# Rank-8 channel scales multiplied as float32r passes, with both operands split in two parts

## The chip, the cores and the metric

The kernel runs on one core of a Trainium2 chip. The core has a matrix engine (TensorE, PE in the profile, with its weight loads shown as PEld), a vector engine (VectorE, DVE), an activation engine (ScalarE, ACT), a general engine (GpSimd, POOL) and SyncE (SP), which here only issues DMAs. Each engine works through its own queue in order and waits on semaphores for the others. The metric is the device time of one execution in microseconds (us); smaller is better.

## The reference

The program takes hidden states x of 4 batches of 512 rows with 1024 features. It normalizes each row, runs causal attention with rotary embedding (16 heads of 64), and multiplies the result by a gate. The gate is a one-layer network with a sign-valued weight whose inputs and outputs are scaled per token and channel; the scales are what the change is about:

```python
xf = x.reshape(-1, H)
router_logits = xf @ gate_w.T
routing = jax.nn.softmax(router_logits.astype(jnp.float32), axis=1).astype(x.dtype)
in_scale = routing @ in_channel_scale
out_scale = routing @ out_channel_scale
wb = ste_sign(weight)
out = xf * in_scale @ wb.T * out_scale + bias
```

The output is `x + attention(xn) * silu(out)`, with `xn` the normalized rows in both places. Each scale matrix is thus a product with a contraction over only eight experts.

## The kernel before

**Stages.** The first and longest stage runs over 16 groups k, that is 4 batches b times 4 groups g of four heads. In each group the projections of query, key and value (`project`, L260, a Strassen scheme of seven products) are interleaved on PE with the attention pieces of the group before: scores, softmax, transposes of the probabilities (`transpose_p`, L432), values. Pieces that belong to other work are put between them: the router in each batch's first group, the sign of two weight blocks there too, the normalization and transposes of the next batch's rows in groups 2 and 3. After that come two units of the gate's feed-forward beside the last attention pieces, and then, for each of the eight units q (a unit is two row blocks of 128, `pairs`), the output projection `project_out(q)` and the feed-forward `gated(q + 1)` in turn.

**Who sets the order.** PE's order is as written (`tc.manual_schedule(engines={PE})`, L69). On the other engines a scheduler of the framework orders the instructions by its own estimate of when they can run; the first batch's opening is written out for DVE and ACT too (L618). Buffers come from pools: a new tile waits until the older tile in its slot has been read. A pool that matters here is `xin` (L113), two row buffers of 128x1024 shared by the next batch's rows (`load_x`) and the weight blocks whose sign is taken (`load_sign`). The PSUM ring (L116) has four banks for products, transposes and scales alike.

**The router** (L471) works per batch in three steps that stand apart in PE's order. Step 0: logits on PE, eight expert columns in a field of 32 for each row block, copied out by ACT (`lgs`). Step 1: a transpose, then maximum, subtraction, exponential (ACT), sum, reciprocal and product (`rex`, L494 to L502); the 24 unused columns of each field are zeroed by POOL (L492). Step 2: a transpose back on PE (L508), a copy (`rT`), and four stores of eight rows by SP to a DRAM tile `rt_d` (L512).

**The scales.** `load_xn(q)` (L535) fetches a unit's normalized rows and its routing `RT[q]`: eight rows of routing in each of the four 32-partition groups, by four SP DMAs (L548). `isc` and `osc` hold the two scale tables, eight rows in each of the four partition groups (L686, L687, loaded early by eight SP DMAs). `in_scales(q)` (L560) makes 16 products of 8x128 by 8x128, four channel blocks j on the four partition groups, and DVE multiplies the rows by them (L577). `split(q)` (L579) takes the scaled rows apart into two float32r tiles, `HI` and `LO`, for the feed-forward (L777). `out_scales(q)` (L592) makes four products of 8x128 by 8x512; ACT copies them out (L606). Both run in float32.

For units 0 and 1 these products stand inside the last four attention groups, where they use the score banks; for units 2 to 7, inside `project_out` of the unit before:

```python
            ahead = [
                lambda: (in_scales(q + 1), split(q + 1)),
                lambda: None,
                lambda: out_scales(q + 1),
            ]
```

On POOL, which the change gives new work, stand the scaling of the probabilities (L400), two steps of the rotary embedding (L253, L254), one addition of the projections (L336), and in the last stage the bias, gate and residual additions (L788, L797, L901, L921) and the output DMAs (L925, L928).

Of the kernel before, what the change touches and what calls it, by code (L numbers as in the profile page):

```python
# [9 lines left out]
F32 = mybir.dt.float32  # L10
F32R = mybir.dt.float32r
AF = mybir.ActivationFunctionType
ALU = mybir.AluOpType
AX = mybir.AxisListType
# [6 lines left out]
B, S, E = 4, 512, 1024  # L21
H, D = 16, 64
NE = 8
P = 128
# [4 lines left out]
TPB = S // P  # L29
HALF = 512  # L30
# [21 lines left out]
def attn_gated_ffn_kernel(  # L52
# [14 lines left out]
    nc = tc.nc  # L67
# [3 lines left out]
    cp = ctx.enter_context(tc.tile_pool(name="const", bufs=1))  # L71
    st = ctx.enter_context(tc.tile_pool(name="stats", bufs=4))
    sgp = ctx.enter_context(tc.tile_pool(name="sign", bufs=1))
    dp = ctx.enter_context(tc.tile_pool(name="spill", bufs=1, space=DRAM))
# [6 lines left out]
        out=mask,  # L81
        in_=mask,
        compare_op=ALU.is_ge,
        fill=MASK_VAL,
        base=0,
        pattern=[[-1, P]],
        channel_multiplier=1,
# [7 lines left out]
    gw = cp.tile([P, NC, 32], F32, name="gw")  # L95
    nc.gpsimd.memset(gw, 0.0)

    isc = cp.tile([P, E], F32, name="isc")
    osc = cp.tile([P, E], F32, name="osc")

    xn_d = dp.tile([B, TPB, P, E], F32, name="xn_d")
    at_d = dp.tile([B, TPB, P, E], F32, name="at_d")

    rt_d = dp.tile([B, TPB, NE, P], F32, name="rt_d")
    sg = [sgp.tile([P, E], F32R, name=f"sg{n}") for n in range(NC)]


# [3 lines left out]
    xip = ctx.enter_context(tc.tile_pool(name="xin", bufs=2))  # L113
    rtp = ctx.enter_context(tc.tile_pool(name="rt", bufs=2))
# [354 lines left out]
    R = {}  # L469

    def router(b, step):  # L471
        if step == 0:
            lg = bank(f"lg_{b}")[:, :P]
            for c in range(NC):
                for t in range(TPB):
                    nc.tensor.matmul(
                        lg[32 * t : 32 * t + 32, :],
                        lhsT=gw[:, c, :],
                        rhs=X[b][:, c, t * P : (t + 1) * P],
                        start=(c == 0),  # L480
                        stop=(c == NC - 1),
                    )
            R["lg"] = st.tile([P, P], F32, tag="r", name=f"lgs_{b}", bufs=2)
            nc.scalar.copy(R["lg"], lg)
        elif step == 1:
            lt = bank(f"lt_{b}")[:, :P]
            nc.tensor.transpose(lt, R["lg"], ident)
            ltg = lt.rearrange("p (t e) -> p t e", e=32)[:, :, :NE]
            nmx = st.tile([P, TPB], F32, tag="rmx", name=f"rmx_{b}")
            nc.vector.tensor_reduce(nmx, ltg, AX.X, ALU.max)  # L490
            ex = st.tile([P, TPB, 32], F32, tag="r", name=f"rex_{b}", bufs=2)
            nc.gpsimd.memset(ex, 0.0)  # L492
            exv = ex[:, :, :NE]
            nc.vector.tensor_tensor(  # L494
                exv, ltg, nmx[:, :, None].to_broadcast((P, TPB, NE)), op=ALU.subtract
            )
            nc.scalar.activation(exv, exv, AF.Exp)
            ssum = st.tile([P, TPB], F32, tag="rsum", name=f"rsum_{b}")
            nc.vector.tensor_reduce(ssum, exv, AX.X, ALU.add)
            rs = st.tile([P, TPB], F32, tag="rrs", name=f"rrs_{b}")  # L500
            nc.vector.reciprocal(rs, ssum)
            nc.vector.tensor_tensor(  # L502
                exv, exv, rs[:, :, None].to_broadcast((P, TPB, NE)), op=ALU.mult
            )
            R["ex"] = ex
        else:
            rt = bank(f"rt_{b}")[:, :P]
            nc.tensor.transpose(rt, R["ex"].rearrange("p t e -> p (t e)"), ident)  # L508
            rT = st.tile([P, P], F32, tag="r", name=f"rT_{b}", bufs=2)
            nc.vector.tensor_copy(rT, rt)  # L510
            for t in range(TPB):
                nc.sync.dma_start(out=rt_d[b, t], in_=rT[32 * t : 32 * t + NE, :])  # L512


    staged = {}

    def load_sign(n):
        staged[n] = xip.tile([P, E], F32, tag="x", name=f"wb_{n}")
        nc.sync.dma_start(out=staged[n], in_=wb[n // 4, n % 4])

    def make_sign(n):

# [12 lines left out]
    def load_xn(q):  # L535
        b, t = pairs[q]
        if q < 2:
            if q == 0:
                XP["first"] = xp.tile([P, 2, 2, NC, P], F32, tag="X", name="xp_01")
            XP[q] = XP["first"][:, q]  # L540
        else:
            XP[q] = xsp.tile([P, 2, NC, P], F32, tag="xp", name=f"xp_{q}")
        for i in range(2):
            nc.sync.dma_start(out=XP[q][:, i].rearrange("p c q -> p (c q)"), in_=xn_d[b, t + 2 * i])

        RT[q] = rtp.tile([P, 2, P], F32, tag="rt", name=f"rt_{q}")
        for j in range(4):
            nc.sync.dma_start(  # L548
                out=RT[q][32 * j : 32 * j + NE, :, :],
                in_=rt_d[b, t : t + 3 : 2].rearrange("t e p -> e t p"),  # L550
            )

# [6 lines left out]

    def in_scales(q, banks=ring_banks):  # L560

        ps = [v.rearrange("p (i r q) -> p i r q", i=2, r=2) for v in banks(f"is_{q}")]
        for r in range(2):
            for i in range(2):
                for j in range(4):
                    p0, c = 32 * j, 4 * r + j
                    nc.tensor.matmul(  # L567
                        ps[j][:, i, r, :],
                        lhsT=isc[p0 : p0 + NE, c * P : (c + 1) * P],
                        rhs=RT[q][p0 : p0 + NE, i, :],  # L570
                        start=True,
                        stop=True,
                    )
        by_j = XP[q].rearrange("p i (r j) q -> p i r j q", j=4)
        for j in range(4):
            xs = by_j[:, :, :, j, :]
            nc.vector.tensor_tensor(xs, xs, ps[j], op=ALU.mult)  # L577

    def split(q):  # L579

# [11 lines left out]
    def out_scales(q, banks=ring_banks):  # L592
        ps = banks(f"os_{q}")
        for n in range(4):
            i, k = n // 2, n % 2
            nc.tensor.matmul(
                ps[n],
                lhsT=RT[q][32 * n : 32 * n + NE, i, :],
                rhs=osc[32 * n : 32 * n + NE, k * HALF : (k + 1) * HALF],
                start=True,  # L600
                stop=True,
            )
        for n in range(4):
            i, k = n // 2, n % 2
            Z[q, i] = z_place[q % 2][i]
            nc.scalar.copy(Z[q, i][:, k * HALF : (k + 1) * HALF], ps[n])  # L606
# [73 lines left out]
    for k, (b, g) in enumerate(groups):  # L680
        pieces = []
        if k > 0:
            pieces, late = attention_pieces(k - 1, late)
        if k == 1:
            for t in range(TPB):
                nc.sync.dma_start(out=isc[32 * t : 32 * t + NE, :], in_=in_scale)  # L686
                nc.sync.dma_start(out=osc[32 * t : 32 * t + NE, :], in_=out_scale)  # L687
        extra = []
        if g == 0:
            extra = [lambda s=s: router(b, s) for s in range(3)]  # L690
        elif g == 1 and b + 1 < B:
            for t in range(2):
                load_x(b + 1, t)
        elif g > 1 and b + 1 < B:
            t0 = 2 * (g - 2)
            for t in range(t0, t0 + 2):
                layernorm(b + 1, t)
            extra = [
                lambda t=t, h=h: transpose_x(b + 1, t, h) for t in range(t0, t0 + 2) for h in range(2)
            ]  # L700
            if g == 2:
                extra.append(lambda: [load_x(b + 1, t) for t in (2, 3)])
        if g == 0:
            extra += [
                lambda: (load_sign(2 * b), load_sign(2 * b + 1)),
                lambda: None,
                lambda: make_sign(2 * b),
                lambda: make_sign(2 * b + 1),
            ]

        step = max(1, (len(pieces) + len(extra)) // (len(extra) + 1))
        for n, e in enumerate(extra):
            pieces.insert(min(len(pieces), (n + 1) * step + n), e)
        if b == B - 1:

            if g < 2:
                load_xn(g)
            if g in (1, 2):
                pieces.insert(3, lambda: in_scales(g - 1, score_banks))
            if g == 3:  # L720
                z_place[0] = [xip.tile([P, E], F32, tag="x", name=f"z0_{i}") for i in range(2)]
                pieces.insert(3, lambda: out_scales(0, score_banks))
        fill = project(b, g) if k else first
        interleave(pieces, fill, 3 * 7 * 4)
        if g == NGRP - 1 and b + 1 < B:
            for n in (1, 2, 3, 4):
                form_x(b + 1, n)
# [88 lines left out]
    w, v = late  # L816
# [193 lines left out]
```

## Time and profile before

| what | us |
|---|---|
| median of 3 runs | 1217.93 (1216.91 to 1218.15) |
| the profiled execution | 1218.51 |
| its span, first to last instruction | 1216.7 |
| in-scale products (L567), 256 records, from start to next matmul at 701.45 | 1.11 |
| out-scale products (L596), 64 records, the same at 806.42 | 1.07 |
| DVE multiplication by the in-scales (L577), one of 32 | 0.68 |
| ACT copy of the out-scales (L606), one of 32, four per unit | 0.60 |
| SP's issue of a routing load (L548), median of 32 | 0.29 |
| SP's issue of a routing store (L512), median of 16 | 0.29 |
| POOL's issue of an output DMA (L925, L928), 16 | 0.57 to 0.77 |

A float32 matmul of the program leaves two records in the trace, a float32r matmul one. A row of the timeline gives the start, the duration of what it merges, the engine, the line, the operation, the tiles and their sizes, and in brackets how long the engine stood idle before it and what released it. Matmuls are pipelined, so their cost is read from one start to the next and not from a record's length.

### The profile page before, as it was taken

The numbers are of one execution on the slowest core, as the hardware profiler recorded it, in microseconds if no ns is written. First come the engines' busy times: TensorE is split into PE (matmuls) and PEld (weight loads), VectorE is DVE, ScalarE is ACT, GpSimd is POOL, SyncE is SP. The second block draws the span as 40 slices with busy tenths as digits, with TensorE's granted clock in tenths as the row PEclk, the third lists the DMA queues.
The fourth block names the chain that finished last, engine by engine and source line by source line (L and its number), as shares of the span: only waits on it lengthen the run. The fifth ranks groups of instructions, "written<-read, shape, count | busy, mean of one in ns | idle before, by whom it ended". The sixth has DMA issues, their size and how long they took to land.

```text
span 1216.7 us, 18118 instructions
## 1 busy us (share of the span) xinstructions
PE 1184.6 (97%) x6920; PEld 897.6 (74%) x6920; DVE 742.2 (61%) x1364; ACT 500.1 (41%) x1142; POOL 526.4 (43%) x566
## 2 busy tenths in 40 slices
PE   6999998999999899999999999999999999999997
PEld 5988887887888788787887888788664546655663
DVE  7775758766665867666786666665675343444432
ACT  3553745446374544447454443545432121212110
POOL 0463436344343545344363524535445434533543
PEclk9999999999999999999999999999999999999999
DMA  8413324122233422214234221210515423341320
GB/s 301 144 70 113 102 90 147 48 75 81 88 111 95 131 79 78 79 48 142 89 100 161 79 78 44 87 45 27 192 33 194 138 72 102 105 139 35 104 70 34
DMA packets 56983, 120.27 MB, mean 99 GB/s; under 512 B 4609, under 2 KB 38017, under 8 KB 50753
## 3 DMA queue, kind: packets, MB, share of 16 engines
q1 hardware_dynamic: 54592, 110.74, 28.0%
q0 software_dynamic: 2304, 8.39, 1.7%
q8 instruction: 54, 0.88, 0.3%
q14 instruction: 33, 0.26, 0.1%
HBM read 93.88 MB, written 25.23 MB: 98 GB/s over the span
## 4 chain that ended last, share of the span: by engine, by line
PE 81%; DVE 9%; ACT 5%; DMA 3%; issue 1%; POOL 1%; POOLq 0%; ACTq 0%; DVEq 0%
PE pj L281 29%; PE wo L889 16%; PE pj L289 10%; PE ff L777 9%; PE ptp L438 5%; PE pv L454 5%; PE sc L372 4%; ACT p L390 1%; DMA x<-in_x 1%; DVE nmx L387 1%; DVE S L230 1%; DVE sg L527 1%; DMA wb<-in_wb 1%; ACT sw L251 1%; PE is L567 1%
## 5 line engine op out<-in xcount | busy, mean ns | idle before, releaser
L400 POOL TENSOR_SCALAR p<-p,rs 128x128 f32<-128x128 f32 (+3 forms) x256 | 175.8, 701 | 187.1 <-DVE rs L398 187.1
L390 ACT ACTIVATE p<-sc,nmx 128x128 f32<-128x128 f32 (+3 forms) x256 | 132.6, 524 | 164.1 <-DVE nmx L387 159.0
L281 PE MATMUL pj<-T,S 128*128 128x256 f32 x768 | 182.8, 380 | 0.7 <-DVE T L242 0.7
L281 PEld LDWEIGHTS pj<-T,S 128*128 128x128 f32 x768 | 139.8, 190 | 19.5 <-issue 2.1
L336 POOL TENSOR_TENSOR part<-part,part 128x256 f32<-128x256 f32 x48 | 37.2, 775 | 219.1 <-ACT part L335 195.9
L281 PE MATMUL pj<-X,w 128*128 128x256 f32 x512 | 126.9, 390 | 0.9 <-DVE v L337 0.9
L253 POOL TENSOR_TENSOR sw<-sw,sin_sb 128x512 f32<-128x512 f32 x64 | 83.5, 1304 | 89.1 <-ACT sw L251 88.8
L438 PE MATMUL ptp<-ident,p 128*128 128x128 f32 x640 | 96.9, 276 | 12.6 <-POOL p L400 9.7
L281 PEld LDWEIGHTS pj<-X,w 128*128 128x128 f32 x512 | 95.5, 196 | 13.5 <-DVE v L337 1.1
L387 DVE TENSOR_REDUCE nmx<-sc 128x2 f32<-128x512 f32 (+3 forms) x128 | 103.5, 819 | 2.2
L777 PE MATMUL ff<-sg,hi 128*128 128x512 f32 x256 | 103.4, 404 | 0.0
L438 PEld LDWEIGHTS ptp<-ident,p 128*128 128x128 f32 x640 | 79.4, 142 | 29.2 <-POOL p L400 11.6
L777 PE MATMUL ff<-sg,lo 128*128 128x512 f32 x256 | 99.8, 390 | 0.0
L444 ACT COPY pT<-ptp 128x512 f32<-128x512 f32 x96 | 56.0, 586 | 104.1 <-PE ptp L438 103.2
L289 PE MATMUL pj<-S,T 128*128 128x128 f32 x768 | 92.1, 277 | 0.0
L250 ACT ACTIVATE sw<-c 32x512 f32<-32x512 f32 x128 | 80.4, 628 | 27.7 <-DVE c L308 25.9
L289 PEld LDWEIGHTS pj<-S,T 128*128 128x128 f32 x768 | 88.1, 192 | 1.7
L254 POOL TENSOR_TENSOR rot<-rot,sw 128x512 f32<-128x512 f32 x64 | 86.7, 1355 | 4.8
L372 PE MATMUL sc<-rot,rot 64*128 64x384 f32 (+3 forms) x512 | 82.2, 450 | 0.0
L251 ACT ACTIVATE sw<-c 32x512 f32<-32x512 f32 x128 | 80.4, 628 | 1.7
L230 DVE TENSOR_TENSOR S<-w 128x512 f32<-128x512 f32 x96 | 73.4, 773 | 6.0 <-PE pj L281 5.2
L454 PE MATMUL pv<-pT,v 128*64 128x256 f32 (+3 forms) x512 | 76.0, 439 | 0.0
(119 smaller groups left out, 1984.1 us busy)
## 6 DMA issues: line engine op xcount, KB each, us to landing
w<-in_wqkv SPq DMA_DIRECT2D x48, 1024.0 KB
x<-in_x SPq DMA_DIRECT2D x16, 512.0 KB
xn_d<-X SPq DMA_DIRECT2D x16, 512.0 KB
at_d<-at SPq DMA_DIRECT2D x32, 256.0 KB
xp<-xn_d SPq DMA_DIRECT2D x16, 512.0 KB
ap<-at_d SPq DMA_DIRECT2D x16, 512.0 KB
xr<-in_x SPq DMA_DIRECT2D x16, 512.0 KB
wb<-in_wb SPq DMA_DIRECT2D x8, 512.0 KB
```

Of the source, the lines that this page charges most:

```text
L251: nc.scalar.activation(sw[r + 32 : r + 64, :], c[r : r + 32, :], AF.Copy, scale=sc)
L254: nc.gpsimd.tensor_tensor(rot, rot, sw, op=ALU.add)
L281: nc.tensor.matmul(ps, lhsT=wq[:, k, :], rhs=xq[:, k, :], start=(k == 0), stop=(k == 3))
L289: nc.tensor.matmul(ps[:, j * P : (j + 1) * P], lhsT=xq[:, k, j * P : (j + 1) * P], rhs=wq[:, k, :], start=(k == 0), stop=(k == 3),)
L372: nc.tensor.matmul(ps[:, h, :], lhsT=Q[u][r : r + D, i * P : (i + 1) * P], rhs=K[u][r : r + D, : (i + 1) * P], start=True, stop=True,)
L387: nc.vector.tensor_reduce(nmx, ps, AX.X, ALU.max, negate=True)
L390: nc.scalar.activation(pt[:, h, :], ps[:, h, :], AF.Exp, bias=nmx[:, h : h + 1], accum_out=ssum[:, h : h + 1],)
L400: nc.gpsimd.tensor_scalar(pt[:, h, :], pt[:, h, :], rs[:, h : h + 1], 1.0, op0=ALU.mult, op1=ALU.mult,)
L438: nc.tensor.transpose(tp[:, k, :], probs(u, i)[:, h, j * P : (j + 1) * P], ident)
L454: nc.tensor.matmul(pv[r : r + D, j * P :], lhsT=V[u][:, j, r : r + D], rhs=PT[u][:, n, o : o + (TPB - j) * P], start=(j == 0), stop=(j == ...
L777: nc.tensor.matmul(acc, lhsT=part[q][:, i, c, :], rhs=sg[4 * k + c // 2][:, (c % 2) * HALF : (c % 2 + 1) * HALF], start=(c == 0 and part i ...
L889: nc.tensor.matmul(ps, lhsT=lhs[:, k, :], rhs=rhs[:, k, :], start=(k == 0), stop=(k == 3))
```

## The change

Each operand of the two scale products is written as a sum of two float32r parts, a high one (the value rounded to float32r) and the rest, and all four products of parts are laid along the contraction: 4 times 8 experts fill the 32 rows of a partition group.

- The router's step 1 makes four blocks of eight columns in `ex`: 0 and 1 hold the high part of the routing, 2 and 3 the rest. There is no memset any more. The stores to `rt_d` and the loads from it have 32 rows instead of 8; `RT` is a float32r tile and is loaded by POOL's queue instead of SP's.
- `isc` and `osc` become float32r tiles. Each table is copied by 16 DMAs of eight rows into a row buffer of the pool `xin`, in the first group of batch 1 (input) and batch 2 (output), and there taken apart: with a mask `is_high`, by partition, the rows alternate between high part and rest.
- `in_scales` makes 8 products of 32x128 by 32x256, `out_scales` 4 of 32x128 by 32x512, all in float32r. In `in_scales` the two row blocks i of a unit lie side by side in one product, and the bank's layout is turned accordingly.

```diff
+    high = cp.tile([P, 8], F32, name="high")
+    nc.gpsimd.memset(high, 1.0)
+    for sign, base in ((1, 0), (-1, 7)):
+        nc.gpsimd.affine_select(
+            out=high,
...
+    is_high = cp.tile([P, 2], F32, name="is_high")
...
-            ex = st.tile([P, TPB, 32], F32, tag="r", name=f"rex_{b}", bufs=2)
-            nc.gpsimd.memset(ex, 0.0)
+            ex = st.tile([P, TPB, 32], F32, tag="r", name=f"rex_{b}", bufs=1)
...
+            hi = st.tile([P, TPB, NE], F32R, tag="rhi", name=f"rhi_{b}", bufs=1)
+            nc.vector.tensor_copy(hi, exv)
+            hi = hi.bitcast(F32)
+            for n in (3, 2):
+                nc.vector.tensor_tensor(
+                    ex[:, :, n * NE : (n + 1) * NE], exv, hi, op=ALU.subtract
+                )
+            for n in (1, 0):
+                nc.vector.tensor_copy(ex[:, :, n * NE : (n + 1) * NE], hi)
...
-                nc.sync.dma_start(out=rt_d[b, t], in_=rT[32 * t : 32 * t + NE, :])
+                nc.sync.dma_start(out=rt_d[b, t], in_=rT[32 * t : 32 * t + 32, :])
...
+    def load_scales(src):
+        staged["scales"] = xip.tile([P, E], F32, tag="x", name="scales")
+        for t in range(P // NE):
+            nc.sync.dma_start(out=staged["scales"][NE * t : NE * (t + 1), :], in_=src)
+
+    def split_scales(dst):
+        v = staged["scales"]
+        nc.vector.tensor_reduce(is_high[:, 0:1], high, AX.X, ALU.max)
+        nc.vector.tensor_scalar(
+            is_high[:, 1:2], is_high[:, 0:1], -1.0, 1.0, op0=ALU.mult, op1=ALU.add
+        )
+        nc.scalar.copy(dst, v)
+        nc.vector.tensor_tensor(v, v, dst.bitcast(F32), op=ALU.subtract)
+        nc.vector.tensor_scalar(v, v, is_high[:, 1:2], None, op0=ALU.mult)
+        nc.vector.scalar_tensor_tensor(
+            dst, dst.bitcast(F32), is_high[:, 0:1], v, op0=ALU.mult, op1=ALU.add
+        )
...
-            nc.sync.dma_start(
-                out=RT[q][32 * j : 32 * j + NE, :, :],
+            nc.gpsimd.dma_start(
+                out=RT[q][32 * j : 32 * j + 32, :, :],
...
-        for r in range(2):
-            for i in range(2):
-                for j in range(4):
-                    p0, c = 32 * j, 4 * r + j
-                    nc.tensor.matmul(
-                        ps[j][:, i, r, :],
-                        lhsT=isc[p0 : p0 + NE, c * P : (c + 1) * P],
-                        rhs=RT[q][p0 : p0 + NE, i, :],
-                        start=True,
-                        stop=True,
-                    )
+        for r in range(2):
+            for j in range(4):
+                rows, c = slice(32 * j, 32 * j + 32), 4 * r + j
+                nc.tensor.matmul(
+                    ps[j][:, r, :, :],
+                    lhsT=isc[rows, c * P : (c + 1) * P],
+                    rhs=RT[q][rows, :, :],
+                    start=True,
+                    stop=True,
+                )
...
-                lhsT=RT[q][32 * n : 32 * n + NE, i, :],
-                rhs=osc[32 * n : 32 * n + NE, k * HALF : (k + 1) * HALF],
+                lhsT=RT[q][32 * n : 32 * n + 32, i, :],
+                rhs=osc[32 * n : 32 * n + 32, k * HALF : (k + 1) * HALF],
...
-        if k == 1:
-            for t in range(TPB):
-                nc.sync.dma_start(out=isc[32 * t : 32 * t + NE, :], in_=in_scale)
-                nc.sync.dma_start(out=osc[32 * t : 32 * t + NE, :], in_=out_scale)
...
+            if b in (1, 2):
+                extra += [
+                    lambda: load_scales((in_scale, out_scale)[b - 1]),
+                    lambda: None,
+                    lambda: split_scales((isc, osc)[b - 1]),
+                ]
```

The three new entries of `extra` also lengthen the list of pieces of the first group in batches 1 and 2, over which the projections' products are spread, so the places of those pieces in PE's order shift by a few matmuls there.

More of the change, by code (lines that the diff above doesn't have):

```diff
@@ L96, in attn_gated_ffn_kernel @@
     nc.gpsimd.memset(gw, 0.0)
-    isc = cp.tile([P, E], F32, name="isc")
-    osc = cp.tile([P, E], F32, name="osc")
+    isc = cp.tile([P, E], F32R, name="isc")
+    osc = cp.tile([P, E], F32R, name="osc")
+    high = cp.tile([P, 8], F32, name="high")
[3 more added lines that the diff above has]
+            out=high,
+            in_=high,
+            compare_op=ALU.is_ge,
+            fill=0.0,
+            base=base,
+            pattern=[[-16 * sign, 8]],
+            channel_multiplier=sign,
+        )
+    is_high = cp.tile([P, 2], F32, name="is_high")
     xn_d = dp.tile([B, TPB, P, E], F32, name="xn_d")
     at_d = dp.tile([B, TPB, P, E], F32, name="at_d")
-    rt_d = dp.tile([B, TPB, NE, P], F32, name="rt_d")
+    rt_d = dp.tile([B, TPB, 32, P], F32, name="rt_d")
     sg = [sgp.tile([P, E], F32R, name=f"sg{n}") for n in range(NC)]
@@ L482, in router @@
                     )
-            R["lg"] = st.tile([P, P], F32, tag="r", name=f"lgs_{b}", bufs=2)
+            R["lg"] = st.tile([P, P], F32, tag="r", name=f"lgs_{b}", bufs=1)
             nc.scalar.copy(R["lg"], lg)
@@ L508, in router @@
             nc.tensor.transpose(rt, R["ex"].rearrange("p t e -> p (t e)"), ident)
-            rT = st.tile([P, P], F32, tag="r", name=f"rT_{b}", bufs=2)
+            rT = st.tile([P, P], F32, tag="rT", name=f"rT_{b}", bufs=1)
             nc.vector.tensor_copy(rT, rt)
             for t in range(TPB):
-                nc.sync.dma_start(out=rt_d[b, t], in_=rT[32 * t : 32 * t + NE, :])
+                nc.sync.dma_start(out=rt_d[b, t], in_=rT[32 * t : 32 * t + 32, :])
     staged = {}
@@ L544, in load_xn @@
             nc.sync.dma_start(out=XP[q][:, i].rearrange("p c q -> p (c q)"), in_=xn_d[b, t + 2 * i])
-        RT[q] = rtp.tile([P, 2, P], F32, tag="rt", name=f"rt_{q}")
+        RT[q] = rtp.tile([P, 2, P], F32R, tag="rt", name=f"rt_{q}")
         for j in range(4):
-            nc.sync.dma_start(
-                out=RT[q][32 * j : 32 * j + NE, :, :],
+            nc.gpsimd.dma_start(
+                out=RT[q][32 * j : 32 * j + 32, :, :],
                 in_=rt_d[b, t : t + 3 : 2].rearrange("t e p -> e t p"),
@@ L560, in in_scales @@
     def in_scales(q, banks=ring_banks):
-        ps = [v.rearrange("p (i r q) -> p i r q", i=2, r=2) for v in banks(f"is_{q}")]
+        ps = [v.rearrange("p (r i q) -> p r i q", i=2, r=2) for v in banks(f"is_{q}")]
         for r in range(2):
-            for i in range(2):
-                for j in range(4):
-                    p0, c = 32 * j, 4 * r + j
-                    nc.tensor.matmul(
-                        ps[j][:, i, r, :],
-                        lhsT=isc[p0 : p0 + NE, c * P : (c + 1) * P],
-                        rhs=RT[q][p0 : p0 + NE, i, :],
-                        start=True,
-                        stop=True,
-                    )
+            for j in range(4):
[6 more added lines that the diff above has]
+                    stop=True,
+                )
         by_j = XP[q].rearrange("p i (r j) q -> p i r j q", j=4)
@@ L576, in in_scales @@
             xs = by_j[:, :, :, j, :]
-            nc.vector.tensor_tensor(xs, xs, ps[j], op=ALU.mult)
+            nc.vector.tensor_tensor(xs, xs, ps[j].rearrange("p r i q -> p i r q"), op=ALU.mult)
     def split(q):
```

## The prediction

> **What bounds the kernel now.** I read the page first (busy time), then TensorE's waits, then the two groups of products that the change rewrites, then the timeline at the few places where TensorE stands still.
>
> ```profile
> PE 1184.6 (97%) x6920; PEld 897.6 (74%) x6920; DVE 742.2 (61%) x1364; ACT 500.1 (41%) x1142; POOL 526.4 (43%) x566
> ```
> ```profile
> PE ptp L438 <- POOL p L400: 9.7, 5, 4.1
> PE xtp L186 <- DVE x L174: 8.6, 2, 8.3
> ```
> PE is busy 97% of the span and waits seldom: 8.6 us at the start, 9.7 us in five waits of the probability transposes, little else. So whatever comes off PE's own queue comes off the span. The scale products are two such lumps, eight times each:
>
> ```profile
> 701.45 1.17 PE L567 MATMUL is<-rt,isc 8*128 8x128 f32 x32
> 702.56 2.42 PE L281 MATMUL pj<-T,S 128*128 128x256 f32 x10
> ```
> ```profile
> 806.42 1.14 PE L596 MATMUL os<-osc,rt 8*128 8x512 f32 x8
> 807.49 2.43 PE L281 MATMUL pj<-T,S 128*128 128x256 f32 x10
> ```
> From the start of a lump to the next matmul: 1.11 us (in-scales) and 1.07 us (out-scales), with PE's work adjoining on both sides. What one pass costs is read from the chain of waits (start, duration, count of records):
>
> ```profile
> 1170.60 14.54 PE ff L777 x64
> 1185.14 24.05 PE wo L889 x56
> ```
> The float32r product ff takes 14.54/64 = 0.227 us per 512 columns, one record a matmul; the float32 product wo 0.429 us per record and two records a matmul, so 0.86 us: four passes. Last, the longest waits of PE, at the start of batches 1 and 2 (the second, at 421.4 us, has the same shape and lasts 4.08):
>
> ```profile
> 199.34 0.69 DVE L162 BATCH_NORM_STATS2 bn<-x 128x6 f32<-128x512 f32 x1 [3.02 <-DMA x<-in_x]
> 202.24 1.28 ACT L166 ACT_TABLE_LOAD   x1
> 203.84 1.28 ACT L390 ACT_TABLE_LOAD   x1
> 207.55 0.65 PE L438 MATMUL ptp<-ident,p 128*128 128x128 f32 x4 [3.70 <-POOL p L400]
> ```
> DVE stood 3.02 us before the statistics of a row block that had not landed, with the row maxima of the softmax behind them; ACT then loaded the square root's table and the exponential's again in the middle of the exponentials. Both ended in PE's 3.70 us. After each of the two waits the clock halves:
>
> ```profile
> 208.80:212.30 3.50, 3.50 (x12) 2.86 (x11) 2.70 (x6) 1.23 (x5) 2.87 (x4) 0.51 0.97 279
> 423.80:430.70 6.90, 5.27 (x17) 4.45 (x18) 6.04 (x12) 3.18 (x12) 5.96 (x7) 0.51 0.49 152
> ```
> (stretch, its length, busy time of PE, PEld, DVE, ACT, POOL, then the granted clock: 0.51.)
>
> **What the Trainium skill says.** "FP8 and Floating Point Precision", TensorE Precision Notes: true FP32 takes four passes; the trace agrees (0.86 against 0.227 us). "TensorE: Matmul & The Clock Gate", Part 3: matmuls on distinct 32-row groups run together, measured at 3.07 times for four; the trace agrees: 16 in-scale matmuls of 128 columns in four passes are 8192 column-passes, 16 x 0.215 = 3.43 us one after another, and took 1.11. The same page, Part 1: an idle window of about 3.4 us brings the clock to half; here both waits above 3.4 us, and no shorter one, were followed by it. "DMA: Bandwidth & Descriptors", SWDGE vs HWDGE vs iDMA: a DMA that casts, also to float32r, must be issued from GpSimd; no run here shows such a DMA.
>
> **The change part by part.**
>
> *Products, all eight units.* Each of the four row groups now streams 4 x 128 columns in four passes, 0.86 us of the 1.11 (0.25 is start and weights), and 512 columns in four passes of the 1.07 (0.21). Afterwards it streams 512 columns in one pass in both: 0.227 + 0.25 = 0.48 and 0.227 + 0.21 = 0.44. Saved: 8 x (0.63 + 0.63) = 10.1 us. Below: if float32r groups don't overlap, 4 x 0.227 + 0.25 = 1.16, nothing saved; above: 12 us, if part of the 0.25, weights loaded 32 times and now 8 times, goes too. In five of the units the fourth bank waits for DVE (L787) to empty the feed-forward's last bank (0.36 us idle); only 6 of the 32 records stand before that wait, so the saving behind it is nearly whole. DVE's multiplications read the same 512 elements a bank (0.68 us) and have some 25 us of wo and ff products before their result is needed.
>
> *The order at batches 1 and 2.* Built, the changed kernel loads the scales through the same two row buffers, between the sign weights and the next batch's rows. So the statistics, the two square roots and their table loads are no longer queued among the softmax at 199 and 417 us, but in the middle of the group, after the split of the scales. Gone: 3.70 + 4.08 = 7.8 us of waiting. Next late would be the first probabilities: without 3.02 us on DVE, 1.57 us of statistics and 2.85 us on ACT they are ready near 202, when PE arrives at 203.85. The half-clock stretches go with the waits: PE lost half of 3.4 us and of 5.3 us (430.7 - 425.4), together 4.3 us. Sum 12.1 us. Next in line is DVE's form_x, last ended at 214.7 for a product at 215.6; it moves 4.6 us earlier, PE 5.4; I take 1 us off: 11.1.
>
> *What comes back there.* Split of the scales, twice: on DVE a 128x1024 subtraction (form_x row, 1.22), a scaling (normalize row, 0.81) and a fused multiply-add (two L527 halves at their shortest, 0.68 each: 1.36), 3.4 us; ACT copies 128x1024, two L444 copies, 1.2 us. DVE stands idle 2.15 + 1.70 us at 232.6 to 237.4, where they are queued, so most lies beside PE's work. With statistics and normalization now there too (4.6 us) DVE falls 3 to 4 us behind until the gaps at 251 to 255; PE has four banks ahead, some 5 us. I charge 0.75 us each, 1.5; ends 0 and 12 (a wait as long as the old ones, with half clock). SP issues 16 scale DMAs of some 0.3 us, 4.8 us each time; the weights behind them are fetched three products ahead.
>
> *Router, batch 0.* Here nothing covers:
>
> ```profile
> 31.74 0.17 DVE L502 TENSOR_TENSOR rex<-rex,rrs 128x32 f32<-128x32 f32 x1
> 32.06 0.30 PE L508 MATMUL rt<-ident,rex 128*128 128x128 f32 x1
> ```
> The transpose starts 0.15 us after the routing is ready. Five small DVE operations join (about 0.1 net each), and in DVE's queue a bank add (0.41), a form_w (0.67) and a rotation (0.68) stand between them: 0.5 + 1.76 less overlaps is about 1.9 us, and PE waits in order with the projections behind it. In batches 1 to 3 the transpose comes 6 us after the routing: 0. The dropped memsets (0.2 us, POOL) were idle-time work: 0.
>
> *Routing loads, POOL instead of SP.* 32 DMAs. Nearest row: POOL's output DMA, 0.57 to 0.77 us to issue, 2.9 to 5.9 to landing; I take 0.7, from 0.4 to 1.5 for small casting pieces. Eight are queued after the rotation that ends near 41.4, ahead of the part add (L336, 41.53), where they hold POOL 5.6 us. Behind them: part add, then 6.1 us of rotations, needed by the scores at 55.16 (57.1 with the router's delay): 41.7 + 5.6 + 0.7 + 6.1 = 54.1. Covered up to 1.07 us each; each 0.1 above costs 0.8. The four of unit 2 wait for out-scales of unit 0 (807.5), then have till 812.67; those of the last stages sit in POOL gaps of 9 us. 0. SP loses 32 issues and eight early scale loads: not on the path, 0.
>
> Sum: -10.1 - 11.1 + 1.5 + 1.9 = -17.8. The profiled execution ran 1218.51 us (span 1216.7): 1200.7. The median is 0.6 below it, 1217.93: 1200.1.
>
> **Rivals.**
> - *No overlap or no single pass at 256 columns in float32r.* For: float32r appears only at 512 columns and full rows. Against: float32 row groups overlap now. Without the 10.1: 1210.
> - *The wait moves.* The late statistics wait for a row block whose buffer the split frees, and two table loads still stand before exponentials. For: it happened twice before. Against: the DVE gaps there, and probabilities needed only in the next group. Without the 11.1: 1211.
> - *Both*: 1221, or about even if one holds in part.
> - *Slower: POOL's issue of casting DMAs.* Place: the eight at 41.7 us, then the four of unit 2. Price 8 x (c - 1.07) + 4 x (c - 1.3) beyond cover; it eats the 17.8 from c = 2.6 us on, 3.5 times the dearest row seen; at 3.2 it is 1225. For: no such DMA was profiled. Against: 32 rows are fewer than the 128 of the output.
>
> **How the numbers follow.** Forecast case 0.63, between 1194 and 1207; products without gain 0.10 (1210); waits moved 0.15 (1211); about even 0.03; slower 0.09 (POOL 0.06, the first two together 0.03). What can be told from no change is 0.2%, 2.4 us. Faster 0.88, same 0.03, slower 0.09. The range 1192 to 1213 takes in the first three cases and the low end of the costs.
>
> **What would show it.** Scale lumps of 0.4 to 0.5 us; no PE wait over 2 us near 200 and 416, clock 1.0 there; one PE wait near 2 us before the router's transpose at 32; POOL's rt DMAs under 1 us. Wrong if the lumps stay near 1 us, or if a PE wait over 3 us with half clock stands in the middle of the first group of batches 1 and 2.

## The result, and the profile after

| | before | after |
|---|---|---|
| median | 1217.42 us (4 runs, 1216.70 to 1218.15) | 1200.31 us (4 runs, 1199.20 to 1200.76) |
| ratio | | 0.9858, 95% interval 0.9841 to 0.9875 |
| span of the profiled execution | 1216.7 us | 1199.1 us |
| mean granted clock | 0.994 | 0.998 |

The forecast was 1200.1 us. A second measurement of the changed kernel, beside the last experiments, gave 1200.13 us (0.9860, 0.9845 to 0.9874). Lines are now those of the changed kernel: in-scales L609, out-scales L638, routing loads L591, transposes of the probabilities L454, their scaling on POOL L416.

The page's first part, then TensorE's waits (us in total, times, longest):

```profile
PE 1169.1 (98%) x6696; PEld 886.8 (74%) x6696; DVE 754.9 (63%) x1394; ACT 496.9 (41%) x1140; POOL 544.6 (45%) x597
```
```profile
PE xtp L202 <- DVE x L190: 8.9, 2, 8.6
PE pj L297 <- DVE v L353: 2.7, 3, 1.2
PE ptp L454 <- POOL p L416: 2.2, 3, 1.4
PE ptp L454 <- DVE z_t L831: 1.8, 1, 1.8
PE rt L533 <- DVE rex L529: 1.5, 1, 1.5
PE is L609 <- DVE z L831: 1.4, 3, 0.5
```

PE is busy 15.5 us less in total. The waits for POOL's probabilities fell from 9.7 to 2.2 us; new are 1.5 us before the router's transpose, and 2.7 us (0.9 before) for the sum `v` of a value projection on DVE.

The two products, from the timeline (start, duration, engine, line):

```profile
692.63 0.51 PE L609 MATMUL is<-rt,isc 32*128 32x256 f32 x8
693.07 0.48 PE L297 MATMUL pj<-T,S 128*128 128x256 f32 x1
```
```profile
796.27 0.51 PE L638 MATMUL os<-osc,rt 32*128 32x512 f32 x4
796.71 0.70 PE L297 MATMUL pj<-T,S 128*128 128x256 f32 x2
```

From start to next matmul 0.44 us each, where it was 1.11 and 1.07. Last, the stretches after the places of the two long waits (stretch, length, busy time of PE, PEld, DVE, ACT, POOL, then the granted clock):

```profile
208.00:212.00 4.00, 4.00 (x77) 3.34 (x76) 4.00 (x5) 0.25 (x1) 0.30 (x1) 1.00 0.51 150
423.00:430.00 7.00, 7.00 (x93) 5.93 (x92) 4.07 (x6) 1.22 (x3) 0.00 (x0) 1.00 0.37 105
```

The clock stays at 1.00 where it was 0.51. The statistics of batch 1, which stood at 199 us among the softmax, now stand in the middle of the group, and the two table loads with them:

```profile
231.76 0.68 DVE L178 BATCH_NORM_STATS2 bn<-x 128x6 f32<-128x512 f32 x1
...
233.39 1.28 ACT L182 ACT_TABLE_LOAD   x1
...
243.45 1.28 ACT L406 ACT_TABLE_LOAD   x1 [1.40 <-DVE nmx L403]
```

Following PE's instructions through both traces, the 17.6 us between the two spans divide so: the 16 lumps of scale products 10.3 (their sums, 21.56 and 11.24 us); the beginnings of batches 1 and 2, 4.6 and 5.3; against this 1.5 at the router of batch 0, and 1.3 at the very end, of which more below. Together 17.4; the other 0.2 us are small shifts of either sign.

### The profile page after: what moved, and what is told of

It is laid out like the page before. It is cut to its first block, busy times and chain, and to the rows that moved or that the text cites. A ratio compares the mean times of both kernels' runs of the same rounds, so it can differ in the third digit from the quotient of the medians.

```text
span 1199.1 us, 17762 instructions
## 1 busy us (share of the span) xinstructions
PE 1169.1 (98%) x6696; PEld 886.8 (74%) x6696; DVE 754.9 (63%) x1394; ACT 496.9 (41%) x1140; POOL 544.6 (45%) x597
## 4 chain that ended last, share of the span: by engine, by line
PE 80%; DVE 11%; ACT 4%; DMA 2%; issue 1%; POOL 1%; POOLq 0%; ACTq 0%; DVEq 0%
PE pj L297 29%; PE wo L933 16%; PE pj L305 10%; PE ff L821 9%; PE ptp L454 5%; PE pv L470 5%; PE sc L388 4%; DVE nmx L403 2%; DVE S L246 1%; ACT p L406 1%; DVE sg L570 1%; DMA wb<-in_wb 1%; ACT sw L267 1%; DMA x<-in_x 1%; ACT sw L266 1%
## 5 line engine op out<-in xcount | busy, mean ns | idle before, releaser
L416 POOL TENSOR_SCALAR p<-p,rs 128x128 f32<-128x128 f32 (+3 forms) x256 | 174.8, 696 | 203.5 <-DVE rs L414 203.3
L297 PE MATMUL pj<-X,w 128*128 128x256 f32 x512 | 123.9, 382 | 2.7 <-DVE v L353 2.7
L297 PEld LDWEIGHTS pj<-X,w 128*128 128x128 f32 x512 | 92.7, 191 | 15.0 <-DVE v L353 3.4
L454 PE MATMUL ptp<-ident,p 128*128 128x128 f32 x640 | 95.4, 273 | 5.1 <-POOL p L416 2.2
L454 PEld LDWEIGHTS ptp<-ident,p 128*128 128x128 f32 x640 | 78.5, 141 | 20.8 <-POOL p L416 3.7
```

The source lines that it names most:

```text
L297: nc.tensor.matmul(ps, lhsT=wq[:, k, :], rhs=xq[:, k, :], start=(k == 0), stop=(k == 3))
L416: nc.gpsimd.tensor_scalar(pt[:, h, :], pt[:, h, :], rs[:, h : h + 1], 1.0, op0=ALU.mult, op1=ALU.mult,)
L454: nc.tensor.transpose(tp[:, k, :], probs(u, i)[:, h, j * P : (j + 1) * P], ident)
```

## Experiments: the two halves of the gain

Losses in this section are counted from the first measurement of the changed kernel, 1200.31 us.

**The order alone.** The kernel before, with its float32 products and old router; only the scales come through the row buffers.

```diff
-        if k == 1:
-            for t in range(TPB):
-                nc.sync.dma_start(out=isc[32 * t : 32 * t + NE, :], in_=in_scale)
-                nc.sync.dma_start(out=osc[32 * t : 32 * t + NE, :], in_=out_scale)
...
+            if b in (1, 2):
+                extra += [
+                    lambda: load_scales((in_scale, out_scale)[b - 1]),
+                    lambda: None,
+                    lambda: nc.scalar.copy((isc, osc)[b - 1], staged["scales"]),
+                ]
```

> Only the order is changed: the kernel before, with its float32 products and its router, but the scales come through the two row buffers at batches 1 and 2 (16 loads, one ACT copy, no split on DVE). Theory (the statistics are kept out of the softmax at 199 and 417 us): the waits of 3.70 and 4.08 us and the half clock go, about 2 us of shorter waits take their place as in the changed kernel, so 10 us are gained: 1207.4 against 1217.4. If the split on DVE, left out here, costs anything, the gain is larger than 10. Rival (the wait only moves, and the whole gain of the change is in the products): 1216 to 1218, with a TensorE wait of 3 us or more somewhere in batches 1 and 2.

Measured: 1206.51 us against 1216.95, ratio 0.9912 (0.9897 to 0.9927): 10.4 us. Its longest waits of PE:

```profile
PE xtp L186 <- DVE x L174: 8.7, 2, 8.5
PE pj L281 <- DVE v L337: 2.0, 3, 0.7
PE ptp L438 <- DVE z_t L794: 1.8, 1, 1.8
PE ptp L438 <- POOL p L400: 1.7, 3, 0.9
```

The two long waits are gone, and the sum `v` stands in their place here too, 0.66 us at 204.0 and at 416.6, with no split anywhere. So what came back in the changed kernel is not the split of the scales, but the next thing DVE owes PE.

**What in the order does it: the row buffer or the three added pieces?** Here the pieces stay, but the scales are loaded by quarters into the routing buffers.

```diff
-        staged["scales"] = xip.tile([P, E], F32, tag="x", name="scales")
+        for n in ns:
+            v = staged["scales", n] = rtp.tile([P, TH], F32, tag="rt", name="scales")
```

> The changed kernel, but the scales are loaded by quarters into the routing buffers instead of the row buffers; the work pieces stay where the change put them in TensorE's order. Theory (it is the occupied row buffer that holds the statistics back): the statistics stand among the softmax again, waits of 3 to 4 us near 200 and 414 us with half clock behind them, and 10 us are lost: 1210 against 1200.3. Rival (what removed the waits is the three added pieces, which shift the projections against the attention pieces in TensorE's order): no wait above 2 us there, 1200 to 1202.

Measured: 1217.91 us, 1.0008 of before (0.9999 to 1.0016), 17.6 us lost and not 10. The waits at 211.3 and 428.5 us are back (3.72 and 3.65 us), as the theory has it. Its profiled execution was the fastest of twelve (1215.16 us), so the trace shows some 15 us of the loss. The scheduler, which now found free buffers, put both splits into batch 0, between 51 and 121 us. There TensorE had no other work to go on with, and this line among its waits is new:

```profile
PE sc L388 <- ACT p L406: 2.6, 1, 2.6
```

Scores waited 2.6 us at 64.6 for exponentials, which themselves waited for row maxima on DVE, behind the split; a transpose waited 1.3 us at 105.7. The clock halved after the first of these, by three windows of the trace (0.88, 0.50 and 0.77 are the granted clock):

```profile
66.00:68.00 2.00, 0.74 (x2) 0.30 (x4) 0.88 (x4) 1.31 (x5) 0.51 (x2) 0.88 0.17 33
68.00:70.00 2.00, 2.00 (x6) 0.84 (x3) 2.00 (x5) 0.92 (x3) 0.42 (x1) 0.50 0.09 25
70.00:72.00 2.00, 2.00 (x8) 1.63 (x7) 1.99 (x4) 1.39 (x5) 0.79 (x2) 0.77 0.00 0
```

The run mixes two causes, so it was repeated with the loads tied to the routing of their own batch:

```diff
             v = staged["scales", n] = rtp.tile([P, TH], F32, tag="rt", name="scales")
+            nc.vector.tensor_copy(v[:, :1], R["ex"][:, 0, :1])
```

> As the run before it with the scales in the routing buffers, but each of these loads must follow the routing of its own batch (one more copy of one column on DVE), so that the two splits cannot move ahead into batch 0. On DVE the statistics stand exactly where the kernel before has them, the splits about where the change has them. Theory (the occupied row buffer holds the statistics back): waits of 3.6 to 4.1 us near 200 and 414 us with half clock, 9 to 11 us lost: 1210 against 1200.3. Rival (the added pieces did it): 1200 to 1202. The waits seen in batch 0 of the run before (2.6 us at 65, 1.3 us at 106) should be gone either way if they came from the splits there.

Measured: 1211.49 us, 0.9947 (0.9932 to 0.9962): 11.2 us lost. Its timeline, with the idle time before an instruction and what ended it in brackets:

```profile
200.51 0.69 DVE L178 BATCH_NORM_STATS2 bn<-x 128x6 f32<-128x512 f32 x1 [2.98 <-DMA x<-in_x]
...
203.41 1.28 ACT L182 ACT_TABLE_LOAD   x1
205.00 1.28 ACT L406 ACT_TABLE_LOAD   x1
208.71 0.72 PEld L454 LDWEIGHTS ptp<-ident,p 128*128 128x128 f32 x4 [3.83 <-POOL p L416]
208.72 1.12 PE L454 MATMUL ptp<-ident,p 128*128 128x128 f32 x4 [3.64 <-POOL p L416]
```
```profile
208.70:212.20 3.50, 3.48 (x11) 2.95 (x12) 2.70 (x7) 1.56 (x7) 2.87 (x5) 0.50 0.71 202
```

This is the chain of the kernel before, link by link: DVE stands 2.98 us before statistics whose rows have not landed, two table loads, a wait of 3.64 us, the clock at 0.50. The waits in batch 0 are gone. The three added pieces stand in this run too, and the waits are back. It is thus the occupied row buffer that keeps the statistics out of the softmax, and not the shifted pieces.

**The products: passes.** Routing rows and scales in float32 instead of float32r, the new layout kept (the low parts are then zero and the four products sum to the plain one).

```diff
-    isc = cp.tile([P, E], F32R, name="isc")
-    osc = cp.tile([P, E], F32R, name="osc")
+    isc = cp.tile([P, E], F32, name="isc")
+    osc = cp.tile([P, E], F32, name="osc")
...
-        RT[q] = rtp.tile([P, 2, P], F32R, tag="rt", name=f"rt_{q}")
+        RT[q] = rtp.tile([P, 2, P], F32, tag="rt", name=f"rt_{q}")
```

> The changed kernel with routing rows and scales in float32 and not float32r: same 32-row contraction, same count of matmuls, same loads; the split leaves a zero in its low parts, so the sum of the four products is the plain float32 product. Theory (the passes carry the gain of the products): lumps back at 1.05 to 1.1 us for both products, 16 x 0.65 = 10.3 us lost: 1210.6. Rival (fewer matmuls and weight loads, 8 instead of 32 in the in-scales, carry it): the in-scale lump stays below 0.8 us and only the out-scales lose, 1205 or less.

Measured: 1210.64 us, 0.9945 (0.9930 to 0.9959), 10.3 us lost, the expected figure. The lumps are 1.08 and 1.07 us, and 1.91 in the five units with the wait for DVE, where the changed kernel has 1.29. The first of them:

```profile
691.50 1.15 PE L609 MATMUL is<-rt,isc 32*128 32x256 f32 x16
692.58 0.48 PE L297 MATMUL pj<-T,S 128*128 128x256 f32 x1
```

The in-scales have a quarter of the matmuls and weight loads that the kernel before had, and a lump is only 0.03 us shorter for it; the rest is passes.

**The products: row groups.** All scale products on the first 32 rows, which hold the same numbers as the others.

```diff
-                rows, c = slice(32 * j, 32 * j + 32), 4 * r + j
+                rows, c = slice(0, 32), 4 * r + j
...
-                lhsT=RT[q][32 * n : 32 * n + 32, i, :],
-                rhs=osc[32 * n : 32 * n + 32, k * HALF : (k + 1) * HALF],
+                lhsT=RT[q][0:32, i, :],
+                rhs=osc[0:32, k * HALF : (k + 1) * HALF],
```

> The changed kernel with all scale products on the first group of 32 rows, which holds the same numbers as the other three; nothing else differs. Theory (four row groups stream beside each other): alone in one group the in-scales take 8 x 256 and the out-scales 4 x 512 columns one after another, 4 x 0.227 + 0.21 = 1.1 us instead of 0.44, so 16 x 0.67 = 10.7 us are lost: 1211. Rival (a lump is start, weights and one pass, and the groups do not matter): lumps of 0.44 to 0.6 us, 1200 to 1203.

Measured: 1209.10 us, 0.9932 (0.9918 to 0.9947), 8.8 us lost. A lump in its timeline:

```profile
691.83 1.21 PE L609 MATMUL is<-rt,isc 32*128 32x256 f32 x8
692.97 2.43 PE L297 MATMUL pj<-T,S 128*128 128x256 f32 x10
```

1.14 us, where 1.1 was expected: without the four groups beside each other a single pass gains nothing. The total fell short of 10.7 because in five units the serial stream hides part of the wait for DVE, so these lumps grew by 0.34 us only (1.29 to 1.63).

## Experiments: what the change still costs

**The router.** The routing is split after its transposition.

```diff
-            hi = st.tile([P, TPB, NE], F32R, tag="rhi", name=f"rhi_{b}", bufs=1)
-            nc.vector.tensor_copy(hi, exv)
-            hi = hi.bitcast(F32)
...
-            nc.vector.tensor_copy(rT, rt)
+            hi = st.tile([P, P], F32R, tag="r", name=f"rhi_{b}", bufs=1)
+            nc.vector.tensor_copy(hi, rt)
+            nc.vector.tensor_tensor(rT, rt, hi.bitcast(F32), op=ALU.subtract)
             for t in range(TPB):
-                nc.sync.dma_start(out=rt_d[b, t], in_=rT[32 * t : 32 * t + 32, :])
+                for n, v in enumerate((hi.bitcast(F32), hi.bitcast(F32), rT, rT)):
+                    nc.sync.dma_start(
+                        out=rt_d[b, t, n * NE : (n + 1) * NE, :], in_=v[32 * t : 32 * t + NE, :]
+                    )
```

> The changed kernel with the routing split into its two parts after its transposition and not before it: the five small DVE operations ahead of the transpose are gone, two (128x128) follow it, and 16 stores of 8 rows replace 4 of 32 rows on SP, each batch. Theory (the wait of 1.48 us before the transpose in batch 0 is on the path): the wait goes below 0.2 us and 1.4 us come off: 1198.9. Rival (PE would only wait for the next thing, the first sums of the projections): wait moved within the first 60 us, 1200.3.

In the changed kernel the timeline shows what stood between the routing and its transpose:

```profile
30.78 0.18 DVE L517 TENSOR_TENSOR rex<-rex,rrs 128x32 f32<-128x32 f32 x1
30.88 0.42 DVE L324 TENSOR_TENSOR c<-pj,part 128x256 f32<-128x256 f32 x1
31.21 0.17 DVE L522 CAST rhi<-rex 128x32 fp32r<-128x32 f32 x1
31.29 0.68 DVE L246 TENSOR_TENSOR S<-w,S 128x512 f32<-128x512 f32 x1
...
32.18 0.68 DVE L268 SCALAR_TENSOR_TENSOR rot<-c,cos_sb 128x512 f32<-128x512 f32 x1
...
33.10 0.30 PE L533 MATMUL rt<-ident,rex 128*128 128x128 f32 x1 [1.48 <-DVE rex L529]
```

Five operations of some 0.15 us, and three larger ones that the scheduler put between them. Measured without: 1198.24 us, 0.9841 (0.9827 to 0.9856), 1.9 us below the repeated measurement; the wait is not in the trace any more, and no other took its place in batch 0.

**The casting loads on POOL.** Each issued three times, to price the slower rival.

```diff
-        for j in range(4):
+        for j in [j for j in range(4) for _ in range(3)]:
             nc.gpsimd.dma_start(
```

> The changed kernel with each of the 32 casting loads of the routing issued three times, all by POOL: 64 more issues of 0.53 to 0.84 us. It prices the slower rival. Theory (the eight early ones are covered up to 1.07 us each, 8.6 us in all, those of unit 2 up to 1.3 each, 5.2 us): the eight take 24 x 0.54 = 13 us, so PE waits about 4.4 us at the first scores near 57 us, the four take 12 x 0.54 = 6.5 us and cost about 1.3 us, the rest is idle time: 1206. Second theory (all of it is hidden in POOL's idle time): 1200 to 1201. Third (nothing is hidden): 64 x 0.6 = 38 us, 1239.

In the changed kernel the eight early loads take 0.59 us each; behind them and one addition POOL stands idle for 3.12 us until ACT has prepared a rotation:

```profile
39.88 4.74 POOL L591 DMA_DIRECT2D rt<-rt_d  x8
44.62 0.75 POOL L352 TENSOR_TENSOR part<-part,part 128x256 f32<-128x256 f32 x1
48.49 1.27 POOL L269 TENSOR_TENSOR sw<-sw,sin_sb 128x512 f32<-128x512 f32 x1 [3.12 <-ACT sw L267]
```

Measured with three times as many: 1211.63 us, 0.9958 (0.9944 to 0.9972), 11.5 us above the repeated measurement. The early ones make the scores at 57 us wait for this rotation, 3.8 us where 4.4 were expected:

```profile
PE sc L388 <- POOL rot L270: 3.8, 1, 3.8
```

The agreement is partly luck. Three of the 24 issues come only after that rotation, and POOL also stands idle, 2.3 us in all, until earlier loads have landed, which it does not do in the changed kernel:

```profile
47.70 1.06 POOL L591 DMA_DIRECT2D rt<-rt_d  x2 [2.06 <-DMA rt<-rt_d]
```

After the wait the clock is at 0.50 for 3 us, 1.5 us more. Unit 2's loads cost nothing visible. Another 4.9 us had been in no theory: they are at the end. (Wait, half clock and end make 10.2 of the 11.5 us; the profiled execution, at 1210.05 us, was the fastest of six.)

After the kernel's last line the trace has DRAIN records of each engine. Those of POOL, in the changed kernel, the tripled one and the kernel before (ns min/median/max, first and last start; the longest of the three begins with POOL's last output DMA, and is called its drain here):

```profile
L1050 POOLq DRAIN  x3: 46/102/4923, 1193.3 to 1198.8; - x3
```
```profile
L1050 POOLq DRAIN  x3: 46/102/9818, 1197.7 to 1208.1; - x3
```
```profile
L1006 POOLq DRAIN  x3: 40/93/3642, 1212.3 to 1216.5; - x3
```

3.64 us without routing loads on POOL, 4.92 with 32, 9.82 with 96, while the last output lands 2.9 us after its issue in all three. The cast is not the cause: in the run with float32 tiles the same 32 loads cast nothing, take as long to issue (0.53 us against 0.54, medians), and the drain is as long:

```profile
L1050 POOLq DRAIN  x3: 46/102/4927, 1202.9 to 1208.3; - x3
```

SP is through 0.1 us before POOL in the kernel before, 1.4 us before it in the changed one, 6.3 in the tripled one; the end of the program waits for POOL. So 1.3 us of the change's own cost stand behind its last instruction.

**By loads or by bytes?** One load a unit instead of four, with the same pieces.

```diff
-        for j in range(4):
-            nc.gpsimd.dma_start(
-                out=RT[q][32 * j : 32 * j + 32, :, :],
-                in_=rt_d[b, t : t + 3 : 2].rearrange("t e p -> e t p"),
-            )
+        nc.gpsimd.dma_start(
+            out=RT[q], in_=rt_d[b, t : t + 3 : 2].rearrange("t e p -> e t p")
+        )
...
-                nc.sync.dma_start(out=rt_d[b, t], in_=rT[32 * t : 32 * t + 32, :])
+                nc.sync.dma_start(
+                    out=rt_d[b, t].rearrange("(j e) p -> e j p", j=4),
+                    in_=rT[32 * t : 32 * t + 32, None, :].to_broadcast((32, 4, P)),
+                )
```

> The changed kernel with one casting load for each unit instead of four: the routing is stored four times (the 4 stores of a batch each write their 32 rows in 4 copies), and one load brings all 128 rows, the same bytes and pieces of 512 B as the four did. Theory (the end of the run waits for POOL, by 0.077 us for each casting load issued before, from the 1.4 us of the changed kernel and the 6.3 us with 96 loads): 24 loads fewer, so POOL is ready before SP, as in the kernel before, and 1.3 us come off at the very end: 1199.0. Rival (it goes by pieces or bytes, not by loads): the 1.4 us stay, 1200.3. By POOL's own queue nothing else changes.

Measured: 1199.28 us, 0.9854 (0.9837 to 0.9872); the 0.9 us to the repeated measurement of the changed kernel are too few to decide by themselves, but the drain does:

```profile
L1051 POOLq DRAIN  x3: 40/102/3943, 1192.9 to 1197.3; - x3
```

1.0 us shorter with the same pieces and bytes, so it goes by the loads: some 0.04 us for each of 8 or 32 beyond the 3.64 us, and 0.064 on average with 96. The 0.077 of the expectation was too steep for few loads, and 0.3 of the 1.3 us stay.

**The in-scales later.** In five units the fourth bank of the in-scales waits for DVE to empty it. Two output products later it should not.

```diff
             ahead = [
+                lambda: None,
                 lambda: (in_scales(q + 1), split(q + 1)),
```

> The changed kernel with in-scales (and the split behind it) two output products later, and out-scales one product pair later, in the last five units. Theory: in those units the fourth bank waits 0.467 us for DVE to empty the last feed-forward bank; two products later it is long empty: 5 x 0.467 = 2.3 us come off: 1198.0. Rival (the split, which starts some 7 us later, becomes late for the feed-forward): waits before ff, 1200 or more.

Measured: 1196.13 us, 0.9825 (0.9811 to 0.9840): 4.0 us below the repeated measurement, not 2.3. The changed kernel, then this one:

```profile
1125.39 0.39 PE L609 MATMUL is<-rt,isc 32*128 32x256 f32 x3
1126.25 0.50 PE L609 MATMUL is<-rt,isc 32*128 32x256 f32 x5 [0.47 <-DVE z L831]
1126.68 1.55 PE L933 MATMUL wo<-wo,ap 128*128 128x512 f32 x3
```
```profile
1128.39 0.51 PE L609 MATMUL is<-rt,isc 32*128 32x256 f32 x8
1128.83 3.70 PE L933 MATMUL wo<-xp,S 128*128 128x512 f32 x8
```

With the wait a lump takes 1.29 us, without it 0.44. The wait accounts for 0.47 of the difference. The other 0.38 us go because three matmuls run alone before it (0.39 us), and the five behind it still take 0.43 us, as much as all eight in one piece. Five times 0.85 is 4.2 us.

**All three mends.** Router, one load a unit, later in-scales.

> The changed kernel with the three mends together: the routing split after its transposition, in-scales and out-scales later in the last five units, one casting load a unit (the parts in the order high, low, high, low, and high, high, low, low on the side of the scales, so that 8 stores a batch write all copies). Theory (they add up): 1.5 + 2.3 + 1.3 less than 1200.3, 1195.2, and with what the first two took off in their own runs (2.1 and 4.2) down to 1192.7. Rival (they share the same time): not below 1196.1, the run with the later in-scales alone.

Measured: 1195.26 us, 0.9821 (0.9806 to 0.9836), the fastest here: 4.9 us below the changed kernel measured beside it. The lower end was missed: the router's 1.48 us are gone, but the second scores now wait 1.17 us at 62.9 for exponentials on ACT, a wait that the router's mend alone did not show. The changed kernel was measured again beside these runs:

> The changed kernel once more, for the size of small differences beside the other two: 1200.3, all theories.

It gave 1200.13 us. Its waits for `v` are 0.67 us at 206.0 and at 418.4, where the first profile had 0.75 and 1.24; such differences of half a microsecond come and go between executions.

## Why the prediction was right

*Products, all eight units* (10.1 us): right by mechanism and size. Lumps of 0.48 and 0.44 us were forecast, both are 0.44 where nothing waits, and 10.3 us were saved. The float32 run shows the passes, the run on one group shows the overlap, and both are needed: the gain is gone without either. That the saving stays behind the wait for DVE held as well; that the wait itself cost more than its idle time was overlooked (lumps of 1.94 us with it and 1.10 without in the kernel before, 1.29 and 0.44 after). The rival without overlap is refuted.

*The order at batches 1 and 2* and *What comes back there* (11.1 less 1.5, so 9.6): 9.9 measured in the traces, and 10.4 by the order alone. Mechanism shown: the row buffer, the statistics, the table loads, the half clock. On the clock the prediction leaned on the Trainium skill, "TensorE: Matmul & The Clock Gate", Part 1, with an idle window of about 3.4 us, and read it as the length of a wait. Waits of 3.64 to 4.70 us fit that, but the wait of 2.61 us at 64.6 in the run with the early splits was followed by half clock too, while those of 1.8 us were not.

What fits all thirteen traces is a grid. Once the clock has become full, it changes only at multiples of 3.41 us until the last matmul: in the kernel before it is full for 194.56 us (57 of them), half for 3.41, full for 211.63, half for 6.83. Half clock followed every one of these stretches in which PE, at full clock, was idle for 2.14 us or more in all, and none with 1.84 us or less. The wait of 3.70 us in the kernel before fell into two stretches, with 1.56 and 2.14 us, and only the second was followed by half clock. So a wait shorter than 3.4 us can do it, and where it falls counts. Where between 1.84 and 2.14 us the limit lies, no run shows.

Two items were right in sum but wrong in name. What is late next is not form_x but DVE's sum `v`, 0.75 and 1.24 us (1 us in all was put down, for form_x). And the split, charged 0.75 each, costs nothing where the change has it: between 207 and 363 us and between 420 and 577 us PE has no wait above 0.1 us, and the order without a split has waits for `v` too, 0.66 us each. In batch 0 the two splits did cost about 4 us of waits (2.6 and 1.3) and half clock, so their price is a matter of place.

*Router, batch 0* (1.9 us): 1.5, by the interleaving that was named: the bank add, the form_w and the rotation stand there as foreseen.

*Routing loads, POOL instead of SP* (0, taken at 0.7 us each, covered up to 1.07): at their place right, 0.59 us each for the early eight, and no wait behind them. The size of the cover is borne out only roughly by the tripled loads, whose 3.8 us of wait hold other things as well. The slower rival would have needed 2.6 us a load (3.4 times the dearest row of 0.77 us, not 3.5). What the step left out is the end: it counted the issue and the landing of each load, and not that POOL has to be through with all of them before the program ends. That is 1.3 us, which were put at nothing, and it makes up for the 0.2 and 0.3 us by which the first two steps were too careful and the 0.4 of the router. That the sum of 17.8 came so near to 17.6 is therefore in part luck.

## What to carry to other kernels

A load through a shared buffer is also a lock: it decides when the next load, and all the work that a scheduler hangs on it, may start; look at what it keeps out as well as what it brings. Price a short wait in the middle of a burst of small matmuls by the whole lump with and without it, not by the idle time that the profile shows. When DMAs are moved to POOL, look at the end of the program too, and issue few large ones, whether they cast or not.

## What was not expected

- POOL's drain at the end grows with the loads that POOL has issued in the whole run: 3.64, 3.94, 4.92 and 9.82 us with 0, 8, 32 and 96 of them, the last of them issued over 100 us earlier, and 4.93 with 32 that do not cast. What POOL does there, no record shows.
- A casting load of 32 rows (32 KB), in the first profile of the changed kernel, took 0.53 to 0.84 us to issue and 2.1 us (median) to landing; one of 128 rows with four times the bytes 0.75 to 1.08 us, and 2.6 us.
- A wait of 2.61 us was enough for half clock. In all traces half clock followed 2.14 us or more of idle time within one stretch of a grid of 3.41 us.
- A wait of 0.47 us among eight small matmuls cost 0.85 us.
